# A three-layer graph kernel on Trainium2: partly filled edge columns gathered in 14 dense packs in layers 2 and 3, with the packs' lists made in layer 1

## The chip, the cores and the metric

The kernel runs on one core of a Trainium2 chip. The metric is the device time of one execution in microseconds; the time of a version is the median over several executions. A core has TensorE (PE), VectorE (DVE), ScalarE (ACT), GpSimd (POOL) and SyncE (SP), each with its own instruction stream, and 16 DMA engines that move data between HBM and on-chip memory. Here POOL issues the gathers (indirect DMAs, in which 128 partitions each fetch one row by an index), and SP issues the plain loads and stores.

## The reference: what is computed

A graph has N = 6250 nodes with 256 features and E = 100,000 directed edges, whose ends are drawn at random. Three attention layers run over it: two of GATv2 (4 heads of 64, every node with a loop to itself), then one of GAT (8 heads of 32, no loops).

```python
def gatv2(x, src, dst, Wl, Wr, att, b):            # src, dst with the loops
    xl, xr = (x @ Wl).reshape(n, 4, 64), (x @ Wr).reshape(n, 4, 64)
    e = leaky_relu(xl[src] + xr[dst], 0.2)
    logits = einsum('ehc,hc->eh', e, att)
    alpha = softmax of logits over the edges of one dst
    return sum over the edges of one dst of alpha * xl[src], + b

h = gatv2(elu(gatv2(x, ..., Wl1, Wr1, att1, b1)), ..., Wl2, Wr2, att2, b2)
x1 = layernorm(x + h)
# layer 3: Wh = x1 W; logits = leaky_relu(s1[src] + s2[dst]); softmax; sum of alpha * Wh[src]
out = layernorm(x1 + gat(x1))
```

## The kernel before, in words

**Plan.** A first stage (0 to 108 us, `make_plan`) sorts the edges by their target, sorts the nodes by falling number of edges, and cuts them into NB = 49 blocks of P = 128 nodes (NP = 6272 with filler). A block's node is a partition; its edges are columns. `columns(E, N, NB)` works out before the run, from the Poisson law of the degrees and 3.5 standard deviations, how many columns each block needs: 25 for block 1 down to 9 for block 48, 27 for block 0 (`held`), whose few longer nodes go a way of their own (`find_few`, `gather_few`, `few_logits`, `few_sum`). The columns of all blocks sum to 803. As the nodes are sorted, a block's last column is often filled only on its first lanes (partitions). Ten such columns are put into three *packs*, with fixed lanes, in which one gather fetches the rows of several blocks' last columns (793 columns and 3 packs are left to gather): (3, 13, 17, 36), (26, 40, 47, 48) and (31, 43). The pack is gathered when its first block is, and `lay_rows` copies its parts to the blocks' row buffers by a DMA on SP; `lack_rows` puts a filler row on the other lanes. A missing edge points at row NP of the table, whose attention columns hold -1.5e38, so that its weight is zero.

While the plan runs, POOL also issues seven gathers of the planner whose result nothing reads (`spare`, line 1261).

**Rows.** A block's gathered rows stand in one to three tiles of the pool `rows` (9 buffers of up to 9 columns; `chunks`). In layers 1 and 2 slot 0 holds the block's own row (the loop). Every column is one indirect DMA on POOL (`gather_rows`, line 1482); a pack is one on line 1454. Layer 1 reads the table `xl1_d` by `sources`; its rows carry in a last column the number of the row in the order of layers 2 and 3, which ACT copies to `spots` after use (line 1866). Layers 2 and 3 read `xl2_d` and `wh_d` by `spots`.

**Layers 1 and 2** are one function, `layer2(i, ...)`. The order of the instructions on each engine is the program's own (`manual_schedule`), with waits where data or buffers need them. For block b the loop does:

- `attend(b)`: `z = max(rows, pr)` for the first tile was already made (`first_z`, line 1821, during block b-1); the other tiles follow (lines 1841, 1844, 1845: maximum, product with the attention vector, sum per head into the logits `lg`). `weights` issues the maximum on DVE (line 1623) and four exponents on ACT (line 1631). In layer 1 ACT then copies the row numbers to `spots`. `behind` runs what block b-1 left: in layer 1 ACT copies the two products `made` (PSUM, pool `pst`, tag `tp`, two buffers) into rows (line 1959) and SP stores them as `xl2_d` and `xr2_d`. Then DVE does `none` on the next block's `pr` (line 1930) and `first_z(b + 1)`.
- `finish` of block b-1 (the ELU in layer 1; the residual and layer norm in layer 2), then the reciprocal and the division of the weights (line 1638 and following).
- `weighted_sum`: the last `few` columns are weighted by ACT, one head of one column an instruction (line 1673), the others by DVE (line 1677); PE adds all columns in PSUM by products with the identity (line 1684). In layer 1 `few` is a third of the columns, in layer 2 two thirds.
- `fetch(b + 2)`: SP loads for block b+4, copies of packed rows that are due (`waiting`), and the gathers of block b+2 on POOL.
- `turns(b + 2, ...)`: PE transposes the block's next features and the finished rows (line 1602), ACT copies the transposes (line 1607), PE makes `pl`, `pr` and the products for the next layer's tables (line 1612).

The pool tag `tp` of `pst` has two buffers, which the transposes, the products `made` and the small products of block 0 share.

**Layer 3** needs no PE: DVE adds the logits (line 2056), weights the rows (line 1706) and sums them (line 1718); POOL gathers block b+1 and scatters the results by `out` (line 2086).

Of the kernel before, what the change touches and what calls it, by code (L numbers as in the profile page):

```python
# [47 lines left out]
def columns(E, N, NB):  # L48
# [48 lines left out]
    return cols, low, high, held, packs  # L97
# [569 lines left out]
def kernel(  # L667
# [22 lines left out]
    cols, low, high, held, packs = columns(E, N, NB)  # L690
# [7 lines left out]
    node_i = plan.tile([P, NB], I32, name="node_i")  # L698
    fits = plan.tile([P, 1], I32, name="fits")
# [11 lines left out]
    with tc.manual_schedule():  # L711
        make_plan(
            tc, x, src, dst, ((wl1, wr1, att1), (wl2, wr2, att2)), (b1, b2), w3, a3,
            cols, low, high, held, packs, node_i, fits, ident, eps, nobody, att, wc, wh, fixed, xl1_d,
            near_d,
        )
        nc.vector.memset(done, 0)
# [4 lines left out]
    with tc.If(ok != 0):  # L722
        with tc.manual_schedule():
            tile_by_degree(
                tc, x, att1, b1, b2, w3, a3, out, [held] + cols[1:], packs, node_i, near_d, ident, eps, nobody,
                xl1_d, att, wc, wh, fixed, done, wl2, wr2, att2,
            )
# [8 lines left out]
def make_plan(  # L736
    ctx, tc, x, src, dst, layers, biases, w3, a3, cols, low, high, held, packs, node_i, fits, ident, eps,
    nobody, att, wc, wh, fixed, xl1_d, near_d,
# [36 lines left out]
    SPARE = 7  # L775
# [483 lines left out]
    spare = one.tile([P, SPARE, LONG], I32, name="spare")  # L1259
    for k in range(SPARE):  # L1260
        nc.gpsimd.indirect_dma_start(
            out=spare[:, k, :], out_offset=None, in_=listed,
            in_offset=bass.IndirectOffsetOnAxis(ap=begin_i[:, k : k + 1], axis=1),
        )
# [12 lines left out]
    counts = one.tile([P, NB], F32, name="counts")  # L1277
# [26 lines left out]
def tile_by_degree(  # L1304
    ctx, tc, x, att1, b1, b2, w3, a3, out, cols, packs, node_i, near_d, ident, eps, nobody,
    xl1_d, att, wc, wh, fixed, done, wl2, wr2, att2,
# [52 lines left out]
    late = consts.tile([P, len(EARLY)], F32, name="late")  # L1359
# [81 lines left out]
    picks = [consts.tile([P, len(packs)], I32, name=f"pick{k}") for k in range(2)]  # L1441
    for pick in picks:
        nc.gpsimd.memset(pick, NP)
    held_rows = {}
# [6 lines left out]
    def gather_pack(b, pool, name, pick, table, width):  # L1451
        q = opens[b]
        held_rows[q] = pool.tile([P, RW], F32, name=name)
        nc.gpsimd.indirect_dma_start(
            out=held_rows[q][:, :width], out_offset=None, in_=table,
            in_offset=bass.IndirectOffsetOnAxis(ap=pick[:, q : q + 1], axis=0),
        )
# [17 lines left out]
    def gather_rows(b, rows, cut, own, table, of, width, j0, j1):  # L1475


        for g, (s0, s1) in zip(rows, cut):
            for j in range(max(s0 - own, j0), min(s1 - own, j1)):
                if j + 1 == cols[b] and b in packed:  # L1480
                    continue
                nc.gpsimd.indirect_dma_start(  # L1482
                    out=g[:, j + own - s0, :width], out_offset=None, in_=table,
                    in_offset=source(of, b, j),
                )

# [83 lines left out]
    def sort_sources(work, ps, b):  # L1570

        n = cols[b]
# [19 lines left out]
        if b + 1 == len(EARLY):  # L1592
            pb = ps.tile([P, b + 1], F32, name="pb", tag="tp")
            nc.tensor.matmul(pb, ones, late, start=True, stop=True)
            bad = work.tile([P, 1], F32, name="bad")
            nc.vector.reduce_sum(bad, pb, axis=AX.X)
            nc.vector.tensor_single_scalar(done, bad, 0.0, op=OP.is_equal)
# [144 lines left out]
    def layer2(i, table, of, width, start, own, finish, follow):  # L1742
# [5 lines left out]
        with ExitStack() as es:  # L1748
# [5 lines left out]
            packp = es.enter_context(tc.tile_pool(name=f"pack{i}", bufs=len(packs)))  # L1754
# [5 lines left out]
            def gather(b):  # L1760
                first = EARLY[b] if b in begun else 0
                rows, cut = begun.pop(b) if first else row_tiles(b, 1)
                if b in opens:
                    gather_pack(b, packp, "pack", picks[i], table, width)
                gather_rows(b, rows, cut, 1, table, of, width, first, cols[b])
                if b in packed:
# [16 lines left out]
            def fetch(b):  # L1783
# [5 lines left out]
                if i == 0 and b + 1 in opens:  # L1789
                    pick_rows(opens[b + 1], picks[0], sources)  # L1790
                while waiting:
# [34 lines left out]
            def attend(b):  # L1826
# [31 lines left out]
                few = min(S // 3, cut[-1][1] - cut[-1][0] - 1) if i == 0 else (2 * S - 2) // 3  # L1858
# [4 lines left out]
                if i == 0:  # L1863
# [3 lines left out]
                    if b in shuts:  # L1867
                        pick_rows(shuts[b], picks[1], spots)
# [15 lines left out]
            if i == 0:  # L1884
                find_few(work, pst)
            gather(0)
# [8 lines left out]
            for b in range(NB):  # L1895
# [21 lines left out]
                if i == 0 and b == len(EARLY):  # L1917
                    load_last()
                if b + 2 < NB and not ahead(b):
# [102 lines left out]
    layer2(0, xl1_d[:, :], sources, W2 + 1, start1, own1, finish1, begin2)  # L2022
    last_weights()
    layer2(1, xl2_d[:, :], spots, W2, start2, own2, finish2, lambda: begin(0, wh_d, A1))

    with ExitStack() as es:
        packp = es.enter_context(tc.tile_pool(name="pack3", bufs=len(packs)))
        work = es.enter_context(tc.tile_pool(name="work3", bufs=3))
        ps = es.enter_context(tc.tile_pool(name="ps3", bufs=3, space=PSUM))
        state = {}  # L2030

        def gather(b):
            first = EARLY[b] if b in begun else 0
            rows, cut = begun.pop(b) if first else row_tiles(b, 0)
            if b in opens:
                gather_pack(b, packp, "pack3", picks[1], wh_d[:, :], A1)
            gather_rows(b, rows, cut, 0, wh_d[:, :], spots, A1, first, cols[b])
            if b in packed:
                lack_rows(b, rows, cut, wh_d[:, :], A1)
                lay_rows(b, rows, A1)  # L2040
# [4 lines left out]
        def attend(b):  # L2045
# [9 lines left out]
            for g, (s0, s1) in zip(rows, cut):  # L2055
# [3 lines left out]
                )  # L2059
            nc.vector.scalar_tensor_tensor(  # L2060
# [101 lines left out]
```

## Time and profile before

| | |
|---|---|
| median of 9 executions | 3820.85 us (3810.21 to 3840.45) |
| profiled execution | 3834.59 us, span 3832.7 us |
| mean granted clock of TensorE | 0.697 |
| plan; layer 1; layer 2; layer 3 | about 0 to 108; to 1461; to 2613; to 3833 us |
| DVE busy | 2721.4 us (71%), 2619 instructions |
| POOL busy | 2483.5 us (65%), 2585 instructions |
| PE busy | 1605.0 us (42%), 5423 instructions |
| ACT busy | 1338.7 us (35%), 5161 instructions |
| gathers of line 1482 in layers 1 and 2 | x1549, 1469.3 us busy, 833.7 us idle ahead of them |
| gathers of line 1482 in layer 3 | x756, 785.6 us busy, 272.2 us idle ahead |
| DVE, maximum, product and sum of `z` (1841 and 1821, 1844, 1845) | 299.6 + 197.9, 496.8, 497.3 us |
| ACT, weighted columns (1673) | x3080, 804.4 us |

The profile is of one execution. Busy times are of the engine's instructions; the time before an instruction in which its engine did nothing is put down to what released it last. A name like `g<-whs_d,near_r` is output and inputs. The page cuts the span into 40 equal slices and gives the busy share of each engine in tenths, and the granted clock (PEclk) in tenths of full speed. An answer by groups has, for each line, the count, the busy time with the mean in ns, and the idle time ahead with what ended it. An answer by waits has the engine and its waiting line, the engine and line that released it, then the sum in us, the number of waits and the longest. A timeline has the start in us, the length, the engine and the instruction, with the wait ahead of it in brackets.

### The profile page before, as it was taken

How to read it: one execution, taken by the hardware profiler on the slowest of the kernel's cores; microseconds unless marked ns; L12 is line 12 of the kernel's file. 1: busy time of each engine (PE TensorE's matmuls, PEld its weight loads, DVE VectorE, ACT ScalarE, POOL GpSimd, SP SyncE). 2: the span in 40 equal slices, each digit the busy share in tenths (PEclk: the TensorE clock that was granted, in tenths of full speed). 3: DMA queues.
4: the chain of work that ended last, by engine and by line, in shares of the span. 5: the costliest groups of instructions: out<-in, count | busy, mean ns of one | idle time of the engine just before them, and what ended most of it. 6: DMA issues, size and time to landing. Idle time of an engine off the chain costs nothing.

```text
span 3832.7 us, 25468 instructions
## 1 busy us (share of the span) xinstructions
PE 1605.0 (42%) x5423; PEld 1153.4 (30%) x5424; DVE 2721.4 (71%) x2619; ACT 1338.7 (35%) x5161; POOL 2483.5 (65%) x2585
## 2 busy tenths in 40 slices
PE   7346666366556773466665666665000000000000
PEld 6224445244445552234333444443000000000000
DVE  7558878477667895678785878895777565666665
ACT  3224434243334452455555666774000000000000
POOL 4656666565466655666666666664777777777774
PEclk8657878677778896688876888887555555555555
DMA  7534334333234443333343444442433333333332
GB/s 217 129 90 108 102 100 107 88 103 92 76 103 104 109 102 93 95 102 106 106 111 105 108 114 112 117 119 77 107 107 102 99 96 96 98 97 99 97 100 57
DMA packets 176464, 397.64 MB, mean 104 GB/s; under 512 B 50924, under 2 KB 93956, under 8 KB 176284
## 3 DMA queue, kind: packets, MB, share of 16 engines
q0 software_dynamic: 120608, 336.86, 33.6%
q1 hardware_dynamic: 54680, 57.74, 5.1%
q10 hardware_dynamic: 1012, 1.32, 0.1%
q8 instruction: 48, 0.79, 0.1%
q14 instruction: 116, 0.94, 0.1%
HBM read 354.60 MB, written 40.42 MB: 103 GB/s over the span
## 4 chain that ended last, share of the span: by engine, by line
POOL 20%; issue 17%; ACT 12%; PE 5%; another core or an unknown queue 5%; DVE 4%; DMA 1%; POOLq 0%; DVEq 0%; ACTq 0%; SPq 0%
POOL g L1482 19%; ACT g L1673 9%; PE acc L1684 4%; POOL out L2086 1%; ACT at L1631 1%; DVE z L1844 1%; DVE z L1841 1%; DVE lg L1845 1%; DMA g<-whs_d,near_r 1%; PE pm L1612 1%; DVE g L1677 0%; DMA g<-xl_d,near_r 0%; ACT xT L1607 0%; ACT sd L1995 0%
## 5 line engine op out<-in xcount | busy, mean ns | idle before, releaser
L1482 POOL DMA_INDIRECT g<-xl_d,near_r x1549 | 1469.3, 949 | 833.7 <-issue 466.5
L1684 PE MATMUL acc<-g,ident 128*128 128x256 f32 x3408 | 1101.8, 476 | 811.7 <-issue 312.6
L1684 PEld LDWEIGHTS acc<-g,ident 128*128 128x128 f32 x3408 | 760.3, 236 | 1144.4 <-issue 383.5
L1482 POOL DMA_INDIRECT g<-whs_d,near_r x756 | 785.6, 1039 | 272.2 <-issue 244.9
L1673 ACT ACTIVATE g<-g,by 128x64 f32<-128x64 f32 x3080 | 804.4, 338 | 430.0 <-issue 413.3
L1845 DVE TENSOR_REDUCE lg<-z 128x28 f32<-128x1820 f32 (+4 forms) x234 | 497.3, 2125 | 8.6 <-issue 0.6
L1844 DVE TENSOR_TENSOR z<-z,at 128x1820 f32<-128x1820 f32 (+4 forms) x234 | 496.8, 2123 | 4.7
L1718 DVE TENSOR_REDUCE acc_v<-weighted 128x256 f32<-128x3584 f32 (+10 forms) x47 | 319.0, 6787 | 22.3 <-remote 9.9
L1841 DVE TENSOR_TENSOR z<-g,pr 128x1820 f32<-128x1820 f32 (+3 forms) x138 | 299.6, 2171 | 17.8 <-ACT few_own L1832 13.1
L1648 ACT ACTIVATE wt<-lg 128x128 f32<-128x128 f32 (+17 forms) x49 | 14.0, 285 | 802.9 <-issue 255.8
L1677 DVE TENSOR_TENSOR g<-g,at 128x256 f32<-128x256 f32 (+8 forms) x185 | 273.7, 1497 | 4.4 <-issue 1.2
L1607 ACT COPY xT<-pt 128x256 f32<-128x256 f32 x147 | 52.3, 373 | 503.5 <-PE pt L1602 302.3
L1706 DVE TENSOR_TENSOR weighted<-g,wt 128x1792 f32<-128x1792 f32 (+4 forms) x111 | 227.1, 2058 | 0.3
L1821 DVE TENSOR_TENSOR z<-g,pr 128x2080 f32<-128x2080 f32 (+4 forms) x96 | 197.9, 2061 | 28.1 <-issue 16.1
L2056 DVE TENSOR_TENSOR lg<-g,s_r 128x56 f32<-128x56 f32 (+4 forms) x111 | 22.8, 215 | 268.7 <-DMA g<-whs_d,near_r 247.8
L1930 DVE MEMSET pr<- 128x4 f32 x49 | 3.0, 62 | 257.6 <-PE pr L1612 137.6
L1631 ACT ACTIVATE at<-lg,top 128x19 f32<-128x19 f32 (+14 forms) x392 | 115.7, 295 | 138.3 <-issue 70.9
L1728 DVE BATCH_NORM_STATS2 stats<-acc 128x6 f32<-128x256 f32 x49 | 21.1, 430 | 140.2 <-PE acc L1684 90.1
L1612 PE MATMUL pm<-wcat,xT 128*128 128x260 f32 x392 | 99.7, 399 | 21.9 <-ACT xT L1607 21.5
L1612 PE MATMUL pl<-wcat,xT 128*128 128x260 f32 x196 | 76.2, 525 | 73.5 <-ACT xT L1607 37.8
L1638 DVE RECIPROCAL den<-den 128x4 f32<-128x4 f32 x98 | 17.0, 174 | 120.2 <-ACT at L1631 80.2
L1612 PEld LDWEIGHTS pm<-wcat,xT 128*128 128x128 f32 x392 | 78.7, 202 | 37.0 <-ACT xT L1607 22.4
(276 smaller groups left out, 1799.2 us busy)
## 6 DMA issues: line engine op xcount, KB each, us to landing
g<-xl_d,near_r POOLq DMA_INDIRECT x1549
g<-whs_d,near_r POOLq DMA_INDIRECT x756
whs_d<-row SPq DMA_DIRECT2D x49, 132.0 KB
xl_d<-row SPq DMA_DIRECT2D x49, 130.0 KB
xr_d<-row SPq DMA_DIRECT2D x49, 130.0 KB
two<-xl_d SPq DMA_DIRECT2D x49, 130.0 KB
two<-xr_d SPq DMA_DIRECT2D x49, 130.0 KB
near_d<-x_all SPq DMA_DIRECT2D x7, 896.0 KB
```

The lines of the kernel that those rows point to most:

```text
L1482: nc.gpsimd.indirect_dma_start(out=g[:, j + own - s0, :width], out_offset=None, in_=table, in_offset=source(of, b, j),)
L1612: nc.tensor.matmul(pm, xT[:, c, :], w[:, c, :], start=c == 0, stop=c == 1)
L1631: nc.scalar.activation(wt[:, :, h], lg[:, :S, h], AF.Exp, bias=top[:, h : h + 1], accum_out=den[:, h : h + 1],)
L1673: nc.scalar.mul(g4[:, t, h, :], g4[:, t, h, :], by[:, s0 + t - a0, h : h + 1])
L1677: nc.vector.tensor_mul(g4[:, :m], g4[:, :m], wt[:, s0 : s0 + m, :].unsqueeze(3).to_broadcast([P, m, H, F // H]),)
L1684: nc.tensor.matmul(acc, ident, g4[:, t], start=False, stop=s0 + t == S - 1 and not more)
L1706: nc.vector.tensor_mul(prod[:, s0 - base : s1 - base, :].rearrange("p t (h d) -> p t h d", h=H), g[:, :n, :F].rearrange("p t (h d) -> p t ...
L1718: nc.vector.reduce_sum(part, prod[:, : s1 - base, :].rearrange("p s f -> p f s"), axis=AX.X)
L1821: nc.vector.tensor_max(z, rows[0][:, :n, :W2], xr[:, None, :].to_broadcast([P, n, W2]))
L1841: nc.vector.tensor_max(z, g[:, :n, :W2], xr[:, None, :].to_broadcast([P, n, W2]))
L1844: nc.vector.tensor_mul(z, z, at[:, None, :].to_broadcast([P, n, W2]))
L1845: nc.vector.reduce_sum(lg[:, s0:s1, :], z.rearrange("p t (h d) -> p t h d", h=H2), axis=AX.X)
```

## The change

The plan of columns gets a second part, `lanes_of`: for every block from 1 on, the columns whose expected fill (less 3.5 standard deviations) is under three quarters of the lanes are taken out as *lane items*: 33 items in 28 blocks (27 of them with a next block). For these sizes the remaining columns, `base`, sum to 770, and the items go, densely, one after another, into K = 14 packs of 128 lanes. How many lanes an item has is counted on the chip: `find_lanes`, once in layer 1, compares the nodes' edge counts with the column numbers, sums over the lanes by a product on PE, makes running sums on DVE and brings them between bounds known before the run. So an item starts at a lane that is a value on the chip (`lane`, an SP register), and may straddle two packs.

In layer 1 all columns are gathered as before (three packs with fixed lanes included). There `place_lanes`, in `attend` of each of the 28 blocks, makes the packs' lists: for each item three small DVE operations and a PE product that moves the row number of each partition to its lane and pack, and then one DVE addition into `pick_f`. Its PSUM tile is of `pst`, tag `tp`. It stands where the second lists of the old packs were filled before, ahead of `behind`.

In layers 2 and 3 the 14 packs are gathered ahead of the blocks 2, 2, 2, 4, 6, 8, 9, 16, 20, 21, 26, 35, 45 and 47 (`gather_packs`), stored whole in `pack_d` in HBM by SP (`keep_packs`), and every item is loaded from there to its column (`lay_lanes`, on SP, the number of lanes being its upper bound `top`) with a filler row on the lanes above (`lack_lanes`). Lanes that hold another item's rows are closed by an addition of -1.5e38 to the logits (`shut_lanes`, one DVE operation in each block with items). Gathers of line 1482's kind and packs together are 796 in each of these layers before, and 784 after.

Besides: the seven idle gathers of the planner go. ACT's share in layer 1 is `2 * S // 5` columns where it was `S // 3` (with the same upper bound, the last tile's columns less one). The pack tiles of layers 1 and 3 come from the pool `two`.

```diff
+def lanes_of(N, NB, mean, pmf, over, sd, cols, low, high):
...
+    for b in range(1, NB):
+        size = min(P, N - P * b)
+        for c in range(low, cols[b]):
+            if min(size, over[c] - 3.5 * sd[c] - P * b) < 0.75 * P:
+                base[b] = min(base[b], c)
+                items.append((b, c))
+                top.append(max(8, min(P, -(-math.ceil(over[c] + 3.5 * sd[c] - P * b) // 8) * 8)))
...
+    K = -(-hi[-1] // P)
+    need = [min(items[i][0] for i in range(len(items)) if hi[i] + top[i] > P * q) for q in range(K)]
...
@@ make_plan
-    spare = one.tile([P, SPARE, LONG], I32, name="spare")
-    for k in range(SPARE):
-        nc.gpsimd.indirect_dma_start(
...
@@ tile_by_degree
         for g, (s0, s1) in zip(rows, cut):
             for j in range(max(s0 - own, j0), min(s1 - own, j1)):
-                if j + 1 == cols[b] and b in packed:
-                    continue
                 nc.gpsimd.indirect_dma_start(
...
+    upon = [max(2, b) for b in need]
...
+    def find_lanes(zp, ps):
...
+        for k, values in enumerate((lo, hi, [0] + top)):
+            i = 0
+            for j in range(1, len(values) + 1):
+                if j == len(values) or values[j] != values[i]:
+                    nc.vector.memset(bound[:, k, i:j], float(values[i]))
+                    i = j
+        for b, own in items_of.items():
+            nc.vector.tensor_scalar(
+                has[:, own[0] : own[-1] + 1], numbers[:, base[b] : cols[b]], counts[:, b : b + 1],
+                None, op0=OP.is_lt,
+            )
+        pn = ps.tile([P, len(items)], F32, name="lane_n", tag="tp")
+        nc.tensor.matmul(pn, ones, has, start=True, stop=True)
+        nc.vector.tensor_scalar(shut, has, -1.0, BIG, op0=OP.add, op1=OP.mult)
...
+        nc.vector.tensor_tensor_scan(
+            at, ones[:, : len(items) + 1], n, 0.0, op0=OP.mult, op1=OP.add
+        )
...
+    def lane(i):
+        _, (v,) = nc.values_load_multi_w_load_instructions(
+            lane_i[:, i : i + 1], engines=[mybir.EngineType.SP], min_val=lo[i], max_val=hi[i],
...
+        )
+        nc.sync.nop()
+        return bass.ds(v, top[i])
+
+    def place_lanes(work, ps, b, rows, cut):
+        own = items_of.get(b)
+        if own is None:
+            return
+        pk = ps.tile([P, K], F32, name="lane_k", tag="tp")
+        for i in own:
+            j = items[i][1] + 1
+            g, s0 = next((g, s0) for g, (s0, s1) in zip(rows, cut) if s0 <= j < s1)
+            value = work.tile([P, 1], F32, name="lane_value", bufs=2)
+            nc.vector.tensor_single_scalar(
+                value, g[:, j - s0, W2 : W2 + 1], -float(NP), op=OP.add
+            )
+            hot_l = work.tile([P, P], F32, name="lane_hot", bufs=2)
+            nc.vector.tensor_scalar(hot_l, numbers, lane_in[:, 0, i : i + 1], None, op0=OP.is_equal)
+            given = work.tile([P, K], F32, name="lane_given", bufs=2)
+            nc.vector.tensor_scalar(
+                given, numbers[:, 1 : K + 1], lane_in[:, 1, i : i + 1], value,
+                op0=OP.is_equal, op1=OP.mult,
+            )
+            nc.tensor.matmul(pk, hot_l, given, start=i == own[0], stop=i == own[-1])
+        nc.vector.tensor_add(pick_f, pick_f, pk)
...
+    def gather_packs(b, pool, pick, table, width):
+        for q in packs_at.get(b, ()):
+            held_rows[q] = pool(q)
+            nc.gpsimd.indirect_dma_start(
...
+    def keep_packs(b, k):
+        for q in packs_at.get(b, ()):
+            nc.sync.dma_start(pack_d[k][q * P : (q + 1) * P, :], held_rows[q][:, : wide[k]])
+
+    def lay_lanes(b, rows, cut, own, k):
+        for i in items_of.get(b, ()):
...
+            nc.sync.dma_start(g[: top[i], j - s0, : wide[k]], pack_d[k][lane(i), :])
...
+    def shut_lanes(b, lg, own, H):
+        if b in items_of:
+            i0, n = items_of[b][0], len(items_of[b])
+            s = lg[:, base[b] + own : cols[b] + own, :]
+            nc.vector.tensor_add(s, s, shut[:, i0 : i0 + n].unsqueeze(2).to_broadcast([P, n, H]))
@@ layer2
-                if b in opens:
-                    gather_pack(b, packp, "pack", picks[i], table, width)
-                gather_rows(b, rows, cut, 1, table, of, width, first, cols[b])
-                if b in packed:
+                if i == 0 and b in opens:
+                    gather_pack(b, pack_tile, picks[0], table, width)
+                gather_rows(
+                    b, rows, cut, 1, table, of, width, first,
+                    base[b] if i == 1 else cols[b] - 1 if b in packed else cols[b],
+                )
+                if i == 1:
+                    lack_lanes(b, rows, cut, 1, table, width)
+                    if b == 1:
+                        waiting.append(lambda: lay_lanes(b, rows, cut, 1, 0))
+                    else:
+                        lay_lanes(b, rows, cut, 1, 0)
+                elif b in packed:
...
+                if i == 1:
+                    gather_packs(b, pack_tile, lane_pick, table, width)
+                    keep_packs(b, 0)
                 while waiting:
                     waiting.pop(0)()
                 gather(b)
...
+                if i == 1:
+                    shut_lanes(b, lg, 1, H2)
-                few = min(S // 3, cut[-1][1] - cut[-1][0] - 1) if i == 0 else (2 * S - 2) // 3
+                few = min(2 * S // 5, cut[-1][1] - cut[-1][0] - 1) if i == 0 else (2 * S - 2) // 3
...
-                    if b in shuts:
-                        pick_rows(shuts[b], picks[1], spots)
+                    place_lanes(work, pst, b, rows, cut)
                 while behind:
                     behind.pop()()
...
             if i == 0:
                 find_few(work, pst)
+                find_lanes(zp, pst)
             gather(0)
...
     layer2(0, xl1_d[:, :], sources, W2 + 1, start1, own1, finish1, begin2)
+    nc.vector.tensor_copy(lane_pick, pick_f)
     last_weights()
...
```

## The prediction

> **What bounds the kernel now.** I read the page first (its 40 slices), then the windows by stage, then the waits of each stage, then the timeline of single blocks. The profiled execution took 3834.59 us, of which 3832.7 are its span; it lies 14 us above the median of 3820.85, so I make the sum as a difference and put it on the median.
>
> The slices show three layers of about 12 slices each and no engine that is full:
>
> ```profile
> DVE  7558878477667895678785878895777565666665
> POOL 4656666565466655666666666664777777777774
> PEclk8657878677778896688876888887555555555555
> ```
>
> The windows (one in layer 1, one in layer 2, one in layer 3) tell the stages apart; the columns are the busy us of each engine, the granted clock, the DMA share:
>
> ```profile
> core 0: us, PE busy (x) PEld busy (x) DVE busy (x) ACT busy (x) POOL busy (x), PEclk, DMA share, GB/s
> ...
> 215.00:700.00 485.00, 298.22 (x1036) 224.74 (x1037) 384.96 (x355) 192.59 (x716) 317.18 (x335) 0.78 0.39 103
> ...
> 2000.00:2600.00 600.00, 376.87 (x1190) 261.38 (x1190) 483.63 (x408) 407.77 (x1599) 387.74 (x409) 0.81 0.41 112
> ...
> 2700.00:3200.00 500.00, 2.65 (x6) 1.51 (x6) 350.82 (x341) 26.75 (x77) 379.13 (x375) 0.50 0.38 102
> ```
>
> In layers 1 and 2 DVE is busy 79 to 81% and POOL 65%; in layer 3 POOL is busy 76%, DVE 70%. The waits of layer 1, of layer 2 and of layer 3 say who ends last:
>
> ```profile
> DVE pr L1930 <- PE pr L1612: 73.6, 9, 34.3
> POOL g L1482 <- ACT g L1673: 30.7, 7, 4.8
> ...
> POOL g L1482 <- PE acc L1684: 101.0, 34, 11.0
> ...
> DVE lg L2056 <- DMA g<-whs_d,near_r: 247.8, 32, 10.8
> ```
>
> Layer 1: POOL waits for row buffers that the arithmetic has not freed, and DVE waits for TensorE's `pr` of the next block. The ring is: DVE's weights, the weighted sum on ACT and PE, the turn of the next features, `pr`, `first_z`, the next weights. Gathers are not in it. Layer 2: the same, POOL waits for PE. Layer 3: DVE waits for gathered rows, so there, and only there, a gather less is time less.
>
> **Gathers.** Working the column plan through for these sizes, layers 2 and 3 issue 796 gathers each now (793 columns and 3 packs) and 784 after (770 and 14 packs): 12 fewer per layer. In layer 1 nothing goes. In layer 3 a gather costs
>
> ```profile
> L1482 POOL DMA_INDIRECT g<-whs_d,near_r x743 | 773.2, 1041 | 246.7 <-issue 241.3 <-DMA g<-whs_d,near_r 3.0 <-DMA out<-y,node_i 0.9
> ```
>
> 1.04 us and 0.30 between two, 1.34 us. Not all 12 count. DVE's waits for rows run from about 2930 to 3690 us (blocks 9 to 42); the last gather starts at 3783.94, but `out` goes last at 3826.82, because DVE has then two and a half blocks left, at 21 us each with hardly a wait for rows. So the lead that POOL has won when block 42 is gathered decides: 736 gathers before, 728 after, 8 x 1.34 = **-11 us**. In layer 2, POOL waits for buffers in nearly every block (193 us in 53 gaps), so 12 gathers less lengthen its waits: between -15 (12 x 1.25) and 0; I take **-2** (the refill at the layer's start), by the row of POOL's waits.
>
> The seven idle gathers of the planner end at 94.86 us, and POOL then waits another 1.54 us for DVE's `moved`: **0**. If DVE were earlier they would cost 9 us.
>
> **Stores and loads of the packs.** Per layer 14 stores, 33 lane loads and 18 filler loads on SP, each lane load behind a register load. SP's own queue has some 1.5 us of issues a block in layer 2. A pack's trip is store and load; the nearest row is SP's load issued at 118.35 us for which DVE waits until 122.78, 4.4 us, so two of them are 9 us after the pack has landed. Behind each pack gather follow 8 to 22 gathers of the same block (over 11 us), and in layer 2 the fetch runs two blocks ahead. Cover enough: **0**; without the cover up to 9 us for each of 12 pack-opening blocks. SP waits with the two table loads and the row store behind it, and these have a block (16 us or more) of slack. In layers 2 and 3, `shut_lanes` adds a small DVE operation (0.2 us, as `few_lg`) in 28 blocks: **+5** in layer 2, where DVE is in the ring, **+1** in the tail of layer 3.
>
> **The picks in layer 1.** This is where the change costs. `place_lanes` stands in `attend` after the exponents are issued and before `none` and `first_z`. For each lane DVE makes three small operations (0.15, 0.28, 0.2 us, as lines 1507, 1500, 1508) and PE multiplies; then DVE adds `pk` and so waits for PE. `pk` is a tile of the pool `pst`, tag `tp`, with two buffers, and at that moment both hold the two products `made` of block b-1, which ACT's `row` copies free only after the four exponents and the copies into `spots`. Behind the waiting add on DVE stand `none`, `first_z` (2 us), the reciprocal, the weights; for them wait ACT, PE and, by the buffers, POOL. Today `first_z` runs while ACT makes the exponents. Block 36, which has a lane:
>
> ```profile
> 1235.34 0.26 DVE L1623 TENSOR_REDUCE top<-lg 128x4 f32<-128x60 f32 x1
> ...
> 1241.08 0.06 DVE L1930 MEMSET pr<- 128x4 f32 x1 [5.49 <-PE pr L1612]
> ...
> 1242.05 0.37 ACT L1959 COPY row<-pm 128x260 f32<-128x260 f32 x1
> ...
> 1243.38 0.17 DVE L1638 RECIPROCAL den<-den 128x4 f32<-128x4 f32 x1
> ```
>
> Now `none` starts at 1241.08. After, `pk` can start when the copy ends, at 1242.42; a trip DVE, PE, DVE takes 0.70 us here:
>
> ```profile
> 116.88 0.15 DVE L1507 TENSOR_TENSOR few_which<-own_number,few_k 128x1 f32<-128x1 f32 x1 [0.70 <-PE few_k L1505]
> ```
>
> and the add 0.16, so `none` at 1243.28: 2.2 us later. In block 42, where DVE does not wait at all today (`none` at 1349.50, first copy ends 1351.75), the same sum gives 3.1 us. Done so for all 24 lane blocks from 3 to 46 it is 66 us (1.3 to 3.7 each, mean 2.75); blocks 2 and 47 add 3 each, block 1, with nothing in `made` yet, 1; block 48 has no `first_z`. **+73 us**. The lower bound is the case that a buffer is free: 0.6 + 0.86 = 1.5 us in 27 blocks, 40 us; the upper that the answers of PE come as late as the waits for `pr` in blocks 6 to 15 (about 5 us): 135. I take 73, by the block rows themselves.
>
> [...] In layer 1 the granted clock is 0.78, so it was halved in some 44% of the time, and PE sits idle 2.9 us between its bias product and the first weighted row (blocks 35 and 36). [...]
>
> **Smaller things in layer 1.** `find_lanes` puts 85 memsets (0.01 us apart in the row of line 1389), 28 independent comparisons (0.1) and some 14 dependent operations (0.2) with one trip to PE before `second_weights`, whose loads wait for DVE's memsets: 8 us; the first `z` starts at 143.59 after a chain through them. Between 0 and 8, **+6**. The ACT share rises by one column of four multiplications in 28 blocks: DVE saves 0.29 us each (2.02 us for 7 columns), -8; where DVE waits for PE behind ACT, 4 x 0.35 = 1.4 us more in 12 of them, +17. I take **0**.
>
> **Sum.** 73 + 6 + 0 + 5 - 2 - 11 + 1 = +72 us: 3834.6 becomes 3906.6, the median 3820.85 becomes **3893 us**. Its own bounds: 40 + 0 - 8 + 0 - 15 - 11 = +6 and 100 + 8 + 17 + 6 - 0 - 7 = +124 (100 is the wait a third larger), 3827 to 3945.
>
> **The rivals.**
> *Faster.* The lane products are answered while DVE would wait for `pr` anyway, so layer 1 pays nothing; then 6 + 6 - 8 - 11 - 11 (half of layer 2's gathers and a bit more) = -18 us, 3803 us. For it: DVE waits for `pr` in some 25 blocks. Against: `pk` comes after `pr` in PE's order, so that wait cannot cover it. It decides when the lane wait falls under 0.5 us a block. 15%.
> *No change.* The scheduler frees a buffer and the trip is 0.86 us with the lane operations under the wait for `pr`: 28 x 0.86 = 24, and 24 + 5 - 8 - 2 - 10 = +9, 3830 us. It also stands for the case that the lanes hold fewer gathers back than planned. 10%.
> *Much slower.* PE's answers are late. In blocks 16, 24, 25 and 29 of layer 1 DVE loses 20 to 49 us because TensorE's counts arrive 1.4 to 4 us apart while its clock is halved for 20 to 40 us on end. If the added pauses make two more such stretches of 45 us, +162: 3983 us. 13%.
> The forecast itself: 62%.
>
> **Chances and range.** About 0.3%, 11 us, is what a measurement here can tell from no change. Faster 0.15, within 0.10, slower 0.75, straight from the cases. The range from 3805 to 3955 leaves out most of the first and the last rival.
>
> **What would show it.** Right: in layer 1 a DVE wait `pick_f <- PE lane_k` in 27 blocks of 2 to 4 us; ACT's `row` copy just before it; layer 1 longer by 60 to 90 us; layer 2 about as long with longer POOL waits for PE; layer 3 some 10 us shorter with 784 gathers and the same 40 us tail. Wrong: `lane_k` answered without a wait, or waits of DVE for lane loads from `pack_d` in layers 2 and 3, or other lengths of the long TensorE stretches in layer 1, which this sum holds constant.

## The result, and the profile after

The changed kernel takes 3920.68 us in the median of 15 executions (3897.22 to 3955.44); the kernel before 3823.84 us (46 executions). The ratio is 1.026, 95% interval 1.024 to 1.028: 97 us slower, where the forecast was 72 us slower, 3893 us, in a range of 3805 to 3955. The profiled execution took 3941.43 us, of which 3939.6 are its span, 107 us longer than the span of before.

By its sum the forecast was right, by its terms it was not. Here is the span cut at DVE's first `z` and at the first maximum (DVE's `top<-lg`) of each layer (both profiles, us):

| part | before | after | difference | forecast |
|---|---|---|---|---|
| start to the first `z` (plan, `find_lanes`) | 143.6 | 228.6 | +85 | +6 |
| layer 1 from its first to layer 2's first maximum | 1338.7 | 1376.0 | +37 | +73 |
| layer 2 to layer 3's first maximum | 1196.9 | 1178.3 | -19 | +3 |
| layer 3 and the end | 1125.9 | 1128.9 | +3 | -10 |

(Some 27 us of the first block, between `z` and maximum, are alike.) The largest single piece was taken for small change. It is seen at once in the slices of the page:

```profile
DVE  7165678866686886677777788897576766666655
POOL 3724556666556653666666666665577777777772
PEclk8566677777787887687877788888555555555555
```

The second slice, from 98 to 197 us, is nearly empty on DVE and PE's clock is at half in it, while POOL works at seven tenths. The windows (busy us of each engine with the instructions in brackets, granted clock, DMA share) show the hole and the stages that answer to those of before:

```profile
core 0: us, PE busy (x) PEld busy (x) DVE busy (x) ACT busy (x) POOL busy (x), PEclk, DMA share, GB/s
115.00:201.00 86.00, 0.00 (x0) 0.00 (x0) 9.03 (x116) 0.00 (x0) 65.01 (x69) 0.50 0.41 108
300.00:785.00 485.00, 258.00 (x940) 201.94 (x941) 356.48 (x364) 168.46 (x654) 271.60 (x288) 0.74 0.35 90
2100.00:2700.00 600.00, 379.94 (x1205) 260.74 (x1204) 488.06 (x422) 404.69 (x1597) 387.33 (x410) 0.83 0.43 115
2800.00:3300.00 500.00, 2.65 (x6) 1.50 (x6) 352.09 (x352) 26.76 (x77) 380.58 (x376) 0.50 0.39 107
```

In 86 us DVE runs 116 small instructions with 9 us of work, PE and ACT none, and POOL gathers on at its usual step (69 instructions, 1.25 us apart). The timeline of DVE there (start, length, instruction, the wait ahead in brackets):

```profile
115.24 0.31 DVE L1554 MEMSET z<- 128x1 f32 x19
116.02 0.11 DVE L1554 MEMSET z<- 128x2 f32 x7 [0.48 <-issue]
116.75 0.06 DVE L1554 MEMSET z<- 128x1 f32 x1 [0.62 <-issue]
...
152.01 0.06 DVE L1554 MEMSET z<- 128x1 f32 x1 [1.35 <-issue]
153.37 0.33 DVE L1557 TENSOR_SCALAR z<-numbers,counts 128x2 f32<-128x2 f32 x1 [1.30 <-issue]
154.78 0.23 DVE L1557 TENSOR_SCALAR z<-numbers,counts 128x2 f32<-128x2 f32 x1 [1.08 <-issue]
...
201.00 0.20 DVE L1563 TENSOR_SCALAR lane_shut<-z 128x33 f32<-128x33 f32 x1 [9.59 <-remote]
```

The first 26 memsets pass within 0.9 us. From then on they come singly or in small groups, 0.70 us apart and later 1.40 (116.02, 116.75, ..., 153.37, 154.78), and the comparisons all start 1.40 us apart where the work of one is 0.22. "Issue" means that the profile shows nothing waited for, "remote" that it names no line that released the wait. The semaphore count of the last comparison reaches PE 9.6 us after it (line 1562 starts at 201.11).

In layer 1 the mechanism that the prediction named is there. A block with one lane, near 1317 us:

```profile
1318.28 0.41 ACT L2058 CAST near_r<-g 128x6 int32<-128x6 f32 x2
1318.60 0.76 ACT L2152 COPY row<-pm 128x260 f32<-128x260 f32 x2
1319.02 0.39 PE L1613 MATMUL lane_k<-lane_given,lane_hot 128*128 128x14 f32 x2
1320.12 0.17 DVE L1614 TENSOR_TENSOR pick_f<-pick_f,lane_k 128x14 f32<-128x14 f32 x1 [5.34 <-PE acc L1834]
1320.29 0.06 DVE L2123 MEMSET pr<- 128x4 f32 x1
1320.49 2.05 DVE L2011 TENSOR_TENSOR z<-g,pr 128x1820 f32<-128x1820 f32 x1
```

PE multiplies `lane_k` when the first of ACT's two copies has freed a buffer, DVE adds, and only then come `none` and `first_z`. The groups (count, busy us, mean ns, idle ahead by releaser) add this up, first of after, then of before:

```profile
L1614 DVE TENSOR_TENSOR pick_f<-pick_f,lane_k 128x14 f32<-128x14 f32 x28 | 4.8, 170 | 219.1 <-PE lane_k L1613 79.5 <-remote 78.4 <-issue 42.0
L2123 DVE MEMSET pr<- 128x4 f32 x49 | 3.0, 62 | 73.2 <-PE pr L1783 38.8 <-remote 17.5 <-DMA g<-xl_d,near_r 8.7
```

```profile
L1930 DVE MEMSET pr<- 128x4 f32 x49 | 3.0, 62 | 257.6 <-PE pr L1612 137.6 <-remote 51.6 <-issue 39.4
```

DVE now stands idle 219 us ahead of the addition that needs `lane_k`, but only 73 ahead of `pr` where it was 258: the new wait takes the place of 184 us of the old one. The net is 35 us, and layer 1 is 37 us longer. Of the 28 waits for `lane_k`, 13 are of 2.2 to 4.0 us, the size that was forecast; eight of more than 10 us make 145 of the 219.

### The profile page after: what moved, and what is told of

It is laid out like the page before. It is cut to its first block, busy times and chain, and to the rows that moved or that the text cites. A ratio compares the mean times of both kernels' runs of the same rounds, so it can differ in the third digit from the quotient of the medians.

```text
span 3939.6 us, 26535 instructions
## 1 busy us (share of the span) xinstructions
PE 1598.8 (41%) x5491; PEld 1160.6 (29%) x5492; DVE 2755.2 (70%) x2933; ACT 1359.5 (35%) x5273; POOL 2447.6 (62%) x2553
## 5 line engine op out<-in xcount | busy, mean ns | idle before, releaser
L1513 POOL DMA_INDIRECT g<-xl_d,near_r x1526 | 1443.0, 946 | 947.0 <-issue 438.8
L1855 PEld LDWEIGHTS acc<-g,ident 128*128 128x128 f32 x3408 | 773.2, 239 | 1110.1 <-issue 365.6
L1844 ACT ACTIVATE g<-g,by 128x64 f32<-128x64 f32 x3192 | 823.3, 337 | 458.2 <-issue 379.7
L1513 POOL DMA_INDIRECT g<-whs_d,near_r x733 | 764.5, 1043 | 252.4 <-issue 224.1
L1889 DVE TENSOR_REDUCE acc_v<-weighted 128x256 f32<-128x3584 f32 (+10 forms) x47 | 319.0, 6787 | 27.7 <-DVE weighted L1877 11.6
L1848 DVE TENSOR_TENSOR g<-g,at 128x256 f32<-128x256 f32 (+7 forms) x185 | 266.2, 1456 | 3.3
L2287 POOL DMA_INDIRECT out<-y,node_i x49 | 51.7, 1055 | 66.7 <-ACT y L1911 44.8
L1783 PE MATMUL pm<-wh_cat,xT 128*128 128x272 f32 x196 | 69.7, 486 | 55.0 <-issue 31.5
L1783 PE MATMUL pl<-wcat,xT 128*128 128x260 f32 x196 | 67.2, 473 | 57.7 <-ACT xT L1778 42.9
```

The costliest lines, as they stand in the source:

```text
L1513: nc.gpsimd.indirect_dma_start(out=g[:, j + own - s0, :width], out_offset=None, in_=table, in_offset=source(of, b, j),)
L1783: nc.tensor.matmul(pm, xT[:, c, :], w[:, c, :], start=c == 0, stop=c == 1)
L1844: nc.scalar.mul(g4[:, t, h, :], g4[:, t, h, :], by[:, s0 + t - a0, h : h + 1])
L1848: nc.vector.tensor_mul(g4[:, :m], g4[:, :m], wt[:, s0 : s0 + m, :].unsqueeze(3).to_broadcast([P, m, H, F // H]),)
L1855: nc.tensor.matmul(acc, ident, g4[:, t], start=False, stop=s0 + t == S - 1 and not more)
L1889: nc.vector.reduce_sum(part, prod[:, : s1 - base, :].rearrange("p s f -> p f s"), axis=AX.X)
```

## The experiments

Three sets, each on a chip of its own, each with the kernel before beside it (3831.51, 3805.06 and 3231.33 us there). Only ratios to that chip's kernel before are compared; differences in us are the ratio's times 3824 in the first two sets, and that chip's own in the third. The changed kernel was measured only in the comparison above, and no profile of the kernel before was kept from the chips of the sets. So a difference to the change, and a length of a layer set against the kernel before, goes across chips, and a profile is one execution.

### First set: whose 97 us?

The burst by itself, in the kernel before:

```diff
                 find_few(work, pst)
+                room = zp.tile([P, T, W2], F32, name="z").rearrange("p t w -> p (t w)")
+                for k in range(85):
+                    nc.vector.memset(room[:, k : k + 1], float(k))
```

> The kernel before with 85 one-column memsets on DVE put where the change has find_lanes, into a z tile that nothing reads then; nothing else of the change. Theory Q (a burst of short DVE instructions beside POOL's gathers fills a queue that then passes one instruction per 0.7 to 1.4 us): the memsets alone take about 37 us as in the profile of the change (115.2 to 152.0), and the first count after them is some 10 us late: first z at 180 to 195 us, 3860 to 3870 us. Theory G (DVE is held until POOL's run of gathers pauses, however many instructions wait): first z at about 225 us, 3905. Theory F (the forecast: memsets are 0.01 us apart): 3825 to 3830.

Measured: ratio 1.0057 (1.0023 to 1.0091), +22 us; the first `z` at 176.2 us, +32.6.

```profile
116.69 0.32 DVE L1888 MEMSET z<- 128x1 f32 x21
117.22 0.06 DVE L1888 MEMSET z<- 128x1 f32 x1 [0.21 <-issue]
117.92 0.13 DVE L1888 MEMSET z<- 128x1 f32 x8 [0.64 <-issue]
118.67 0.06 DVE L1888 MEMSET z<- 128x1 f32 x1 [0.63 <-issue]
...
138.50 0.06 DVE L1389 MEMSET two<- 128x1 f32 x1 [0.65 <-issue]
150.42 0.42 DVE L1403 TENSOR_TENSOR two<-two 128x256 f32<-128x256 f32 x1 [11.87 <-issue]
```

The steps appear in the kernel before as soon as it has such a burst, again after some 20 instructions. The whole kernel loses less than the start does; in this profile layer 1 took 1308.6 us, 30 less than in that of the kernel before, with the same work (DVE busy 985.5 against 985.7 us). The memsets take 18 us instead of the 37 expected; POOL's gathers go on, so theory G (held until POOL pauses) falls, and the forecast's 0.01 us a memset falls too.

The opposite, in the changed kernel:

```diff
-        for k, values in enumerate((lo, hi, [0] + top)):
-            i = 0
-            for j in range(1, len(values) + 1):
-                if j == len(values) or values[j] != values[i]:
-                    nc.vector.memset(bound[:, k, i:j], float(values[i]))
-                    i = j
+        for k, value in enumerate((0, hi[-1], P)):
+            nc.vector.memset(bound[:, k, :], float(value))
```

> The changed kernel with the 85 memsets of find_lanes replaced by three (the bounds of the lanes are 0, the largest upper bound and 128 for all items; for these inputs the lanes come out the same). The 28 comparisons stay. Theory Q: about 45 DVE instructions are left in this stretch, near the 42 that passed freely before the steps of 0.7 us began, so of the 85 us stall 5 to 40 stay: 3840 to 3875 us. Theory G: the stall lasts until POOL pauses, 3910 to 3920. Theory F: 3915.

Measured: 1.0031 (1.0001 to 1.0061), +12 us. 82 memsets less take 88 of the 99 us that 1.026 stands for. The 28 comparisons now take 3.5 us together, the first `z` is at 159.8. Theory Q is right in kind: the price hangs on the burst, and the 31 instructions that are left of it, some 0.12 us apart, pass without a step.

Place of the addition in layer 1:

```diff
-                    place_lanes(work, pst, b, rows, cut)
                 while behind:
                     behind.pop()()
+                given = place_lanes(work, pst, b, rows, cut) if i == 0 else None
...
                     first_z(b + 1)
+                if given is not None:
+                    nc.vector.tensor_add(pick_f, pick_f, given)
```

> The changed kernel with place_lanes behind ACT's copies of the products, and its DVE addition behind first_z, so that DVE does not wait for lane_k ahead of first_z. Theory F (the lane waits are the price, 66 us): 3850 to 3860 us, layer 1 as long as before. Theory Q (find_lanes is most of the price, and layer 1 is only 37 us longer by the profile): minus 20 to 37, 3884 to 3900.

Measured: 1.0127 (1.0069 to 1.0185), +49 us, so 51 us less than the change (interval some 23 either way), layer 1 at 1349.4 us. That lies between the two theories, and the profile shows 27 us less in layer 1; its execution, of 3915.64 us, was 27 us slower than the median of the six. With the late start, then, the addition ahead of `first_z` was dear; the second set measures its place again, with an early start.

Without picks:

```diff
-                    place_lanes(work, pst, b, rows, cut)
```

> The changed kernel without the calls of place_lanes: the packs of layers 2 and 3 then fetch filler rows only; find_lanes stays. Theory F: layer 1 some 70 us shorter, 3850 us. Theory Q: the picks cost at most the 37 us that layer 1 is longer, 3884 or more; the stall of 85 us at the start of layer 1 is unchanged.

Measured: 1.0053 (1.0021 to 1.0084), +20 us: the picks cost 79 us (some 14 either way). Layer 1 is 1297.7 us, 78 less than with them, and 41 less than before; layers 2 and 3 are as long as with them (1178.0 and 1128.6 us). Of the 78, 20 are DVE's own work (998.5 against 978.6 us busy) and 58 idle time. So leaving the picks out gives back what the forecast said, 73, and layer 1 is otherwise shorter than in the profile of before. Theory Q's "at most 37" was wrong.

### Second set: do the prices add, and what else moved?

> The changed kernel with three memsets in find_lanes instead of 85, and without the calls of place_lanes (the packs of layers 2 and 3 then fetch filler rows only). Theory S (the two prices add up: the late start costs 85, the picks 77 as between the change and no_picks): 3765 us, layer 1 at some 1280 us. Theory O (they overlap: a late start is partly given back by layer 1, which was 41 us shorter than before in no_picks and 30 in burst_before; with an early start the picks cost only some 30): 3805 to 3820, layer 1 at 1320 to 1335.

(The two edits above together.) Measured: 0.9887 (0.9831 to 0.9943), -43 us. Between the two theories: the picks cost 55 us here (24 either way) with an early start, 79 with a late one. Layer 1 is 1292.6 us, so its being 46 us shorter than in the profile of before does not come from a late start.

```diff
-                few = min(2 * S // 5, cut[-1][1] - cut[-1][0] - 1) if i == 0 else (2 * S - 2) // 3
+                few = min(S // 3, cut[-1][1] - cut[-1][0] - 1) if i == 0 else (2 * S - 2) // 3
```

> The changed kernel with three memsets, and ACT's share in layer 1 at a third of the columns as before. Forecast's theory (the share is worth 0, between a gain of 8 and a loss of 17): within 10 us of three_memsets, 3842. Rival: the greater share takes 2 us of DVE from 28 blocks where DVE is in the ring, so that without it the kernel is some 15 us slower, 3857.

Measured: 1.0013 (0.9985 to 1.0042), 7 us less than three_memsets with intervals that overlap: the share is worth nothing that shows, as forecast.

```diff
-                    base[b] if i == 1 else cols[b] - 1 if b in packed else cols[b],
+                    cols[b] if i == 1 else cols[b] - 1 if b in packed else cols[b],
...
-                if i == 1:
-                    gather_packs(b, pack_tile, lane_pick, table, width)
-                    keep_packs(b, 0)
...
-                if i == 1:
-                    shut_lanes(b, lg, 1, H2)
```

> The changed kernel with three memsets, and with layer 2 gathering all its 803 columns one by one (no packs, stores, loads or closing of lanes there); layer 3 keeps its packs. Theory P (layer 2 is 19 us shorter in the change because of its 12 gathers less, against the forecast's 2): layer 2 at 1197 to 1210 us, 3860 to 3875. Theory N (it is shorter for another reason, as the stalls at its start): 3842, layer 2 at 1180.

Measured: 1.0113 (1.0076 to 1.0149): 31 us slower than three_memsets (some 18 either way). Layer 2 is 1188.1 us against 1178.8 there and 1166.6 to 1174.4 in the three other runs of its own chip. So the packs shorten layer 2: 19 gathers for 9 to 22 us of layer 2 by the profiles, each worth 0.5 to 1.1 us of its 1.25.

The cure for both prices, memsets at the start of the plan and the late addition:

```diff
+    for k, values in enumerate((lanes[3], lanes[4], [0] + lanes[1])):
+        i = 0
+        for j in range(1, len(values) + 1):
+            if j == len(values) or values[j] != values[i]:
+                nc.vector.memset(bound[:, k, i:j], float(values[i]))
+                i = j
     SEGS, STEP, BITS = 17, 3, 6
```

> The changed kernel with the 85 memsets moved to the start of the plan (where no gather runs) and the addition of the picks behind first_z. Theory Q (the steps of 0.7 us belong to short instructions beside POOL's gathers): the memsets take 1 to 6 us there in all, first z at 150 to 165 us, and 3800 to 3820 us, about the kernel before. If short instructions come in steps of 0.7 us everywhere: the plan is 30 us or more longer, 3840.

Measured: 0.9996 (0.9967 to 1.0024): the kernel before, to the resolution of this. The same memsets and comparisons:

```profile
0.81 1.75 DVE L822 MEMSET bound<- 128x1 f32 x61 [0.81 <-PEq L2352]
2.97 0.72 DVE L822 MEMSET bound<- 128x1 f32 x24 [0.40 <-issue]
...
110.57 3.67 DVE L1557 TENSOR_SCALAR z<-numbers,counts 128x2 f32<-128x2 f32 x28
```

85 memsets in 2.9 us where no gather runs (in the profile of after the first one starts at 34.44 us), 28 comparisons in 3.7 us beside gathers but without the burst ahead of them; the first `z` at 146.4 us, 3 us later than before. The two moves took 88 us (the memsets, left out) and 51 us each alone, and 101 together.

Set beside three_few_third, which ran on the same chip with the addition in its old place, this run measures that place again, with an early start: 0.9996 against 1.0013, 7 us (some 15 either way), of which 4 lie ahead of the first `z`. The groups, first of three_few_third, then of this run:

```profile
L1610 DVE TENSOR_TENSOR pick_f<-pick_f,lane_k 128x14 f32<-128x14 f32 x28 | 4.8, 170 | 181.4 <-PE lane_k L1609 67.5 <-issue 67.4 <-remote 31.8
L2119 DVE MEMSET pr<- 128x4 f32 x49 | 3.0, 62 | 78.4 <-PE pr L1779 30.0 <-issue 21.3 <-remote 21.1
```

```profile
L2070 DVE TENSOR_TENSOR pick_f<-pick_f,lane_k 128x14 f32<-128x14 f32 x28 | 4.8, 170 | 68.5 <-remote 54.9 <-PE acc L1834 6.1 <-PE lane_k L1613 4.0
L2125 DVE MEMSET pr<- 128x4 f32 x49 | 3.0, 62 | 173.1 <-PE pr L1783 103.4 <-remote 30.5 <-issue 26.2
```

The wait for `lane_k` falls by 113 us and the wait for `pr` grows by 95; DVE's idle time in the whole of layer 1 is 335 and 332 us. So the 51 us of the first set did not come again: with an early start the wait ahead of `first_z` is hardly a price of its own. Layer 1 is still 37 us longer here than in three_no_picks on this chip (1330.0 against 1292.6), 19 of them DVE's work.

### Third set: small terms of the kernel before, and a better version

The chip of this set runs the kernel before in 3231 us, and there the steps do not occur (last section); its numbers speak for that chip.

```diff
-    spare = one.tile([P, SPARE, LONG], I32, name="spare")
-    for k in range(SPARE):
-        nc.gpsimd.indirect_dma_start(
...
```

> The kernel before without the planner's seven idle gathers; nothing else. Forecast: 0, the layers as before. Theory E (what POOL does between its last scatter and the end of the span depends on the number of its DMAs: 1.6 us with 2513 of them, 9.2 us with 2482, 11.1 us with 2501): with 2506 either some 11.6 us, and the kernel 10 us slower, or again under 2 us, and no change.

Measured: 1.0031 (1.0019 to 1.0043), +10 us. The idle gathers are not idle in their effect. POOL's last scatter, in the kernel before, in the kernel before without them, and in the changed kernel:

```profile
3826.82 0.99 POOL L2086 DMA_INDIRECT out<-y,node_i  x1 [8.22 <-DVE y L2128]
```

```profile
3222.69 0.99 POOL L2080 DMA_INDIRECT out<-y,node_i  x1 [8.45 <-DVE y L2122]
```

```profile
3926.03 0.99 POOL L2287 DMA_INDIRECT out<-y,node_i  x1 [8.59 <-DVE y L2329]
```

From its start to the end of the span: 16.0 us without the idle gathers (span 3238.7), 13.5 in the changed kernel (3939.6), but 5.9 in the kernel before (3832.7). The difference lies in two closing instructions of POOL, 2.4 and 9.2 us against 0.5 and 1.1. With 2513 indirect DMAs the end takes 5.9 to 6.1 us in the four profiled kernels that have that number; with 2482 it takes 13.5 to 13.8 in eight, with 2501 15.5, with 2506 16.0. The 11.6 us that theory E gave for the two closing instructions came out. Between 2482 and 2506 the end grows by some 0.1 us for each DMA. But all four kernels with 2513 hold the idle gathers and none of the others does, so whether the number or these gathers themselves make the end short is not separated.

```diff
-                few = min(S // 3, cut[-1][1] - cut[-1][0] - 1) if i == 0 else (2 * S - 2) // 3
+                few = min(2 * S // 5, cut[-1][1] - cut[-1][0] - 1) if i == 0 else (2 * S - 2) // 3
```

> The kernel before with ACT's share in layer 1 at 2 * S // 5; nothing else. Forecast: 0, between -8 and +17 us. Theory L (the share is why layer 1 is 41 to 46 us shorter than before in the two runs without picks): layer 1 at 1295 to 1310 us, 30 to 40 us faster.

Measured: 1.0002 (0.9993 to 1.0011). No effect; theory L falls for this chip.

```diff
-                    if b in shuts:
-                        pick_rows(shuts[b], picks[1], spots)
```

> The kernel before without the loads on SP that fill the second lists of the old packs in layer 1 (blocks 36, 43 and 48; the three packs of layers 2 and 3 then fetch filler rows). If these loads hold SP's queue, they are why layer 1 is shorter in the runs without picks: layer 1 at 1300 us, 30 us faster. If not: no change.

Measured: 1.0000 (0.9991 to 1.0009). No effect either.

The lists summed in PSUM over all blocks, with DVE reading them once:

```diff
-            both = ps1.tile([P, W2 + (CM + 1) * H2], F32, name="at")
+            both = ps1.tile([P, W2 + (CM + 1) * H2 + K], F32, name="at")
+            pk = both[:, W2 + (CM + 1) * H2 :]
...
-            nc.tensor.matmul(pk, hot_l, given, start=i == own[0], stop=i == own[-1])
-        nc.vector.tensor_add(pick_f, pick_f, pk)
+            nc.tensor.matmul(pk, hot_l, given, start=i == 0, stop=i + 1 == len(items))
...
                     new()
+                if i == 0:
+                    place_lanes(work, pk, b, rows, cut)
...
             turns(NB, finish(work, pst, NB - 1, acc)())
             behind.pop()()
+            if i == 0:
+                nc.vector.tensor_add(pick_f, pick_f, pk)
```

> The changed kernel with the 85 memsets at the start of the plan, and with the lists of the packs summed by PE in one PSUM tile over all 28 blocks and read by DVE once, after layer 1; the three DVE operations and the product of each item stand behind the weights. DVE then waits for no lane_k. If that wait is the price of the picks: layer 1 at 1295 to 1310 us as without picks, 25 to 35 us faster than the kernel before. If the operations themselves or the counts that they send are the price: layer 1 at 1325 to 1340 us, within 10 us of the kernel before.

Measured: 0.9971 (0.9961 to 0.9982): 9 us faster than the kernel before on that chip, the one version with packs that clearly beats it. Layer 1 is 1078.9 us (1081 to 1085 in the three kernels of the set that are the kernel before but for one edit), layer 2 980.7 (993 to 995), and 7.5 us are lost again at the end (13.6 against 6.1). Which of the two theories holds stays open: their times were worked out for the slower chips, and the changed kernel and the kernel without picks were not run on this one. DVE is busy for 978 of 1081 us of layer 1 here in before_few_two_fifths, with 2.5 us of waits for `pr`, so the waits that the theories speak of are hardly there to be saved.

## Why the prediction was right, and where its steps failed

**`find_lanes`, +6: the step that failed.** It priced 85 memsets at the 0.01 us apart of three memsets in line 1389, and 28 comparisons at 0.1, and put the end of the range at 8 us. The first `z` came 85 us later, and taking 82 memsets away gave 88 us back. The row it rested on showed three instructions, not eighty-five. But the profile of before does show the step: of ACT's weighted columns (line 1673), some 440 of 2950 starts follow the one before by 0.7 or 1.4 us where 0.24 is the rule. The prediction saw that "counts arrive 1.4 to 4 us apart" and held it to be PE's alone.

**The picks, +73: right in size, the mechanism shown in part.** They cost 79 and 55 us by leaving them out. The chain is as told, down to ACT's copy ahead of `lane_k`, and nearly half of the waits have the size that was forecast. But the sum took the waits as the whole price. DVE's own work makes 20 us of it, and the place of the addition is worth 51 us with the late start and 7 with the early one, so how much of the price is the wait ahead of `first_z` stays open. The faster rival said that the wait for `pr` could cover the wait for `lane_k`; 184 of 219 us did change places in the profile, but the price by leaving the picks out shows that this cover was not free. The sum's own upper end took 100 us for this term, though 135 had been named as its upper bound.

**What the sum did not have, -41.** Layer 1 without picks is 41 to 46 us shorter than in the profile of before, in two runs. DVE's work is 7 us less (978.6 against 985.7 us in layer 1), the 8 us that the forecast gave ACT's share; the other 34 are idle time. It is not the late start (three_no_picks starts early). On the third chip neither the share nor the second lists of the old packs moved the time, but that chip does not show the steps (31 us of idle time ahead of ACT's weighted columns, 430 in the profile of before). Part of it may lie in the base: burst_before, which has nothing of the change, has a layer 1 that is 30 us shorter, too, and the profile of before holds a single wait of 49.1 us where the longest in any other profile of the first two sets is 28.9. How much is left for the change stays open.

**The granted clock, no term of the sum: rightly.** The granted clock of layer 1, from its first maximum to that of layer 2, is 0.77 before and 0.76 after, so no run here shows a price of it.

**Layer 2, -2 + 5: mis-sized.** It went down by 19. POOL's waits for buffers were taken as proof that gathers are not the limit; three_packs_l3_only shows that about half or more of a gather's 1.25 us counts. In the profile after, no DVE instruction waits for a load from `pack_d`, so the 0 for stores and loads of the packs held. `shut_lanes` costs 0.17 us each, as forecast.

**Layer 3, -11 + 1.** The last `out` comes 4.6 us earlier against layer 3's first maximum, and 7.6 us are lost behind it. So the gathers brought some 5 us of the 11; why not more was not tested. The loss belongs to "the seven idle gathers: 0": the term looked at when POOL needed the result, not at the end of the span.

**The much slower rival** (two more late stretches of PE, of 45 us) did not come as such: DVE's longest wait in layer 1 is 28.8 us, against 49.1 before. That 97 lay so near to 72 is luck, a sum of errors: +79 and -36 in the first two rows of the table, -22 and +13 in the others.

## What to carry to other kernels

Price a series of instructions by a row with as many of them, beside the same traffic, not by the spacing of three: here 85 memsets cost 2.9 us in one place and, with what they held up, 85 in another. Put constants and other bursts where no gathers run. Letting PE add up over blocks what DVE needs only once spares DVE a wait in each block, though what that alone is worth was not measured here. Before work is removed because nothing reads its result, look at the end of the span as well as at the place where it stood.

## What the hardware showed that was not expected

**Steps of 0.70 us.** On the chips of the first two sets, and in the profiles of before and after, short instructions of DVE and ACT come at times 0.70 us or a multiple of it apart with nothing waited for (in bounds_early_picks_late, on the second chip, 569 waits of ACT without a cause ahead of its weighted columns, 432 us in all), and a count arrives late, by 9.6 us, behind the burst above. On the chip of the third set this is gone. The group of ACT's weighted columns on the page of the kernel before, and on that of before_few_two_fifths there (which has one column more in 28 blocks):

```profile
L1673 ACT ACTIVATE g<-g,by 128x64 f32<-128x64 f32 x3080 | 804.4, 338 | 430.0 <-issue 413.3 <-DVE by L1640 8.2 <-DVE near_r L1586 3.3
```

```profile
L1673 ACT ACTIVATE g<-g,by 128x64 f32<-128x64 f32 x3192 | 771.6, 336 | 31.2 <-DVE by L1640 31.0
```

430 us of idle time ahead, 413 of them without a cause, against 31; and 593 us less for the whole kernel. The granted clocks (0.70 and 0.71) are alike.

What slows these chips is open. Of a burst, the first 26 memsets in the changed kernel and the first 21 in burst_before pass within 0.9 and 0.4 us, and the rest come, singly or in small groups, in steps of 0.70 us or a multiple of it. No view shows what holds them, so the queue that theory Q names was the author's guess.

**The end of the span** took 5.9 to 6.1 us with the seven idle gathers and 13.5 to 16.0 without them, more with more indirect DMAs on POOL (2482 to 2506), as told under before_no_spare.
